# Fetching the rows of the output sum earlier, and moving one-time transfers from SyncE to GpSimd, in a fused attention and feed-forward kernel

## The chip, the cores and the metric

The kernel runs on one core of a Trainium2 chip. The metric is the time of one execution on the device in microseconds (us). A core has five engines that run side by side, each with its own list of instructions in a fixed order: TensorE (PE in the profile, PEld for its weight loads), VectorE (DVE), ScalarE (ACT), GpSimd (POOL) and SyncE (SP), which here only issues transfers. Each engine executes its list in order, so an instruction that waits holds up those behind it on its engine. A framework places the program's instructions on these lists: it draws the waits from what each instruction reads and writes, hands out the buffers of a pool, and may put an instruction earlier than the source has it when its engine and its buffer are free.

## What is computed

The input x has the shape (2, 2048, 256). It is normalised by layer, and attention and a feed-forward net with ternary weights are both applied to the normalised rows; their outputs are added to x.

```python
xn = _layernorm(x, axis=-1)
x = x + _L0_attn_ref(xn, Wq, Wk, Wv, Wo) + _L0_ffn_ref(xn, ...)
# attention: causal, one head of 256, softmax(q k^T / 16) v Wo
# feed-forward, with _tlin(x, w, s) = (x @ w.T) * s and w in {-1, 0, 1}:
h = silu(_tlin(x, w1_w, w1_s)) * _tlin(x, w2_w, w2_s)      # 256 -> 1024
h = gelu(_tlin(h, h1_w, h1_s))                             # 1024 -> 1024
h = gelu(_tlin(h, h2_w, h2_s))                             # 1024 -> 1024
return _tlin(h, w3_w, w3_s)                                # 1024 -> 256
```

## The kernel before

The 4096 rows are cut into eight blocks of 512. The attention part comes first (to about 277 us of the span). It leaves in device memory, for each block, the transposed normalised rows (`xT_d`) and the attention output (`r_d`). Beside it VectorE makes the factors of the first square layer h1, described below, and the weights are looked through; a flag says whether all are whole small numbers. With such weights, as here, the branch `ffn_ternary` runs (from line 691), and all that the change touches is in it. The other branch `ffn` does not run.

**Rounds.** `ffn_ternary` takes two blocks at a time, n and n + 1, in four rounds. In each round `first` computes the gated first layer (TensorE's L736; ScalarE L741 and VectorE L742 empty the banks), then `square` is called twice, for h1 and h2, and then the last layer w3 (L918) is computed for block n + 1 and then block n, with the outer addition (L924, L925) and the transfer out (L926).

**Square layers.** A layer of 1024 by 1024 is computed by seven products in place of eight, from sums and differences of the weight's quarters and of the inputs. `STEPS` lists the seven pairs; the left members (factors) S1 to S4 are sums of weight quarters, A11, A12 and A22 are quarters themselves. A product is 32 matmuls of 128x128 by 128x512 in the trace's groups on L780. The right members are sums of the round's activations: T1 and T2 by VectorE (L756, L762), the two others by GpSimd (L761, L817), each then split into a rounded part (ScalarE, L719) and a rest (VectorE, L720). L762 overwrites what L761 reads, so it follows L761. The results of products are kept or added up by L791, L800 and L801. All eight PSUM banks are in use: the banks of the first layer are those of products 1 and 2.

**Factors.** The factors lie in device memory, in `factors["h1"]` and `factors["h2"]`, seven pieces of 1 MB. `fetch_factors` (the transfers of L885, issued by SyncE) keeps three fetched tiles ahead, so a new fetch can leave when the product three places earlier has ended. The factors of h2 are made within the first round only: `make_h2(c)`, for c from 0 to 3, loads two chunks of 512 KB (L847), forms four sums on GpSimd (L151), and stores them (L851), 1 MB in 512 pieces of 2 KB. It has two staging slots (tag `stg`) and one buffer of sums (tag `sums`, 8 KB per partition), so the next chunk's sums follow the store's landing. `copy_h2` copies the quarters from place to place in device memory (L860), and `load_w3` loads w3 in two chunks (L855) and rounds it on GpSimd (L132). The dictionary `later` says behind which stage of the first layer or which product of h1 each of these is put; `beside` takes it from there:

```python
later = {
    "B11": lambda: make_h2(0), "B12": lambda: copy_h2(0), "B22": lambda: make_h2(1),
    0: lambda: copy_h2(5), 1: lambda: make_h2(2), 2: lambda: copy_h2(6),
    3: lambda: make_h2(3), 5: lambda: load_w3(0), 6: lambda: load_w3(SC // D),
}
```

**Rows of the outer sum.** Behind the second `square`, for each of the round's two blocks, SyncE fetches the attention output (`rt`, L905) and the rows of x (`xt`, L907), 512 KB each, and GpSimd adds them (L908). Each of `rt` and `xt` has one buffer (`bufs=1`), so the fetch of one block's `rt` waits until the block before has been added up. Each of four groups of 128 rows is then scaled into a tile `yt` (L924, three buffers), `rt` is added to it (L925), and `yt` is sent out (L926).

All of these transfers, L847, L851, L855, L860, L885, L905, L907 and L926, and the fetches of the transposed rows (L708) are in SyncE's one list.

Of the kernel before, what the change touches and what calls it, by code (L numbers as in the profile page):

```python
# [9 lines left out]
F32 = mybir.dt.float32  # L10
# [10 lines left out]
P = 128  # L21
# [41 lines left out]
def attn_ffn_kernel(  # L63
# [73 lines left out]
    def rows(n, t):  # L137
        return ds((n % NB) * TB + t * P, P)
# [553 lines left out]
    def ffn_ternary(actx):  # L692
# [13 lines left out]
        def load_xh(n):  # L706
            t = xh1 if n % 2 else xh0
            nc.sync.dma_start(out=t.bitcast(F32).rearrange("p c h t -> p (c h t)"), in_=xT_d[n])  # L708
# [14 lines left out]
        def first(n):  # L723

            B = {k: [None] * HK for k in ("B11", "B12", "B21", "B22")}
            sets = {"B11": [], "T1": [], "B22": [], "T2": []}
            for k in ("B11", "B12", "B22", "B21"):
                xh = xh1 if k[2] == "2" else xh0
                for i in range(HK):
                    o = i + (HK if k[1] == "2" else 0)  # L730
                    name = f"w_{n}_{k}_{i}"
                    p1, p2 = banks(name, 2)
                    for p, w in ((p1, w1_sb), (p2, w2_sb)):
                        for c in range(DC):
                            for a in range(2):
                                nc.tensor.matmul(  # L736
                                    out=p, lhsT=w[:, c, ts(o, P)], rhs=xh[:, c, a, :],
                                    start=(c == 0 and a == 0), stop=(c == DC - 1 and a == 1),
                                )
                    f = B[k][i] = raw(f"f_{name}")  # L740
                    nc.scalar.activation(f, p1, AF.Silu, scale=sc["w1"][:, o : o + 1])  # L741
                    nc.vector.scalar_tensor_tensor(  # L742
                        f, p2, sc["w2"][:, o : o + 1], f, ALU.mult, ALU.mult
                    )
                    if k == "B11":
                        sets[k].append(split(f, f"{n}_{k}_{i}"))
                    elif k == "B12":
                        t1(B, sets, f"{n}", i)
                    elif k == "B22":
                        b22(B, sets, f"{n}", i)  # L750
                beside(k)
            return B, sets


# [9 lines left out]
        def t2(B, sets, name, i):  # L764
            sets["T2"].append(split(B["B22"][i], f"{name}_T2_{i}"))

        def square(layer, n, B, sets, last):

            name = f"{layer}_{n}"
            s = sc[layer]  # L770
            C, nxt = {}, {k: [] for k in ("B11", "B12", "B21", "B22", "T1", "T2")}

            def product(step, out, start):
                right = STEPS[step][1]
                fetch_factors()
                w = factor_tiles.pop(0)
                for o in range(HK):
                    for c in range(HK):
                        for a in range(2):
                            nc.tensor.matmul(  # L780
                                out=out[o], lhsT=w[:, c, ts(o, P)], rhs=sets[right][c][:, a, :],
                                start=(start and c == 0 and a == 0), stop=(c == HK - 1 and a == 1),
                                skip_group_check=True,
                            )
                if layer == "h1":
                    beside(step)

            def kept(banks, k):
                r = [raw(f"k_{name}_{k}_{o}") for o in range(HK)]
                for o in range(HK):  # L790
                    nc.scalar.copy(r[o], banks[o])  # L791
                return r

            def summed(k, banks, r):

                C[k] = r or [raw(f"f_{name}_{k}_{o}") for o in range(HK)]
                for o in range(HK):
                    at = o + (HK if k[1] == "2" else 0)
                    if r:
                        nc.vector.tensor_tensor(r[o], banks[o], r[o], ALU.add)  # L800
                    nc.scalar.activation(  # L801
                        C[k][o], r[o] if r else banks[o], AF.Gelu, scale=s[:, at : at + 1]
                    )
                    if last:
                        nxt[k].append(split(C[k][o], f"{name}_{k}_{o}"))

            X = banks(f"{name}_X", HK)
            product(0, X, True)
            u1 = kept(X, "u1")
            sets["T3"] = [split(B["B12"][i], f"{name}_T3_{i}") for i in range(HK)]  # L810
            Z = banks(f"{name}_Z", HK)
            product(1, Z, True)
            p5 = kept(Z, "p5")
            for i in range(HK):

                t4 = B["B22"][i]
                nc.gpsimd.tensor_tensor(t4, B["B21"][i], t4, ALU.subtract)  # L817
            sets["B21"] = [split(B["B21"][i], f"{name}_B21_{i}") for i in range(HK)]
            product(2, X, False)
            u2 = kept(X, "u2")  # L820
            sets["T4"] = [split(B["B22"][i], f"{name}_T4_{i}") for i in range(HK)]
            product(3, Z, False)
            summed("B12", Z, u2)
            product(4, X, False)
            summed("B22", X, p5)
            Y = banks(f"{name}_Y", HK)
            product(5, Y, True)
            summed("B11", Y, u1)
            if not last:
                for i in range(HK):  # L830
                    nxt["B11"].append(split(C["B11"][i], f"{name}_B11_{i}"))
                for i in range(HK):
                    t1(C, nxt, name, i)
                for i in range(HK):
                    b22(C, nxt, name, i)
            product(6, X, False)
            summed("B21", X, None)
            if not last:
                for i in range(HK):
                    t2(C, nxt, name, i)  # L840
            return C, nxt

        def make_h2(c):
            halves = []
            for k in (c, c + HK):
                t = stgp.tile([P, SC], F32, tag="stg", name=f"stgt_h2_{k}")
                nc.sync.dma_start(out=t, in_=h2[:, k, :])  # L847
                halves.append(t)
            sums = stgp.tile([P, 4, HB], F32, tag="sums", name=f"sums_h2_{c}", bufs=1)
            sums_of_factors(sums, halves, range(4))  # L850
            nc.sync.dma_start(out=factors["h2"][:, 1:5, c, :], in_=sums)  # L851

        def load_w3(c):
            t = stgp.tile([P, SC], F32, tag="stg", name=f"stgt_w3_{c}")
            nc.sync.dma_start(out=t, in_=w3[:, c : c + SC // D, :].rearrange("p c d -> p (c d)"))  # L855
            rounded(w3_sb[:, c : c + SC // D, :].rearrange("p c d -> p (c d)"), t)

        def copy_h2(step):
# [8 lines left out]
            3: lambda: make_h2(3), 5: lambda: load_w3(0), 6: lambda: load_w3(SC // D),  # L867
        }
        assert HK == 4 and HC == 2 * SC // D

        def beside(at):
            if at in later:
                later.pop(at)()


        factor_order = [
# [4 lines left out]
        def fetch_factors():  # L881
            while factor_order and len(factor_tiles) < 3:
# [5 lines left out]
                )  # L888
                factor_tiles.append(w)

        load_xh(1)
        fetch_factors()

        for n in range(0, N, 2):
# [3 lines left out]
            if n + 2 < N:  # L898
                load_xh(n + 2)
                load_xh(n + 3)  # L900
            B, sets = square("h1", n, B, sets, False)
            B, sets = square("h2", n, B, sets, True)
            for m in (n + 1, n):
                rest = op.tile([P, NT, D], F32, tag="r", name=f"rt_{m}", bufs=1)
                nc.sync.dma_start(out=rest, in_=r_d[m].rearrange("p (t d) -> p t d", d=D))  # L905
                xt = op.tile([P, NT, D], F32, tag="x", name=f"xt_{m}", bufs=1)
                nc.sync.dma_start(out=xt, in_=rows_of(m))  # L907
                nc.gpsimd.tensor_tensor(rest, rest, xt, ALU.add)  # L908
                h = sets["B11"] + sets["B21"] if m == n else sets["B12"] + sets["B22"]
                ys = banks(f"y_{m}", NT)  # L910

# [4 lines left out]
                for t, c in order:  # L916
                    for a in range(2):
                        nc.tensor.matmul(  # L918
                            out=ys[t][:, :D], lhsT=h[c][:, a, ts(t, P)], rhs=w3_sb[:, c, :],
                            start=(c == 0 and a == 0), stop=(c == HC - 1 and a == 1),  # L920
                        )
                    if c == HC - 1:
                        y = op.tile([P, D], F32, tag="y", name=f"yt_{m}_{t}")
                        nc.vector.tensor_tensor(y, ys[t][:, :D], s3, ALU.mult)  # L924
                        nc.vector.tensor_tensor(y, y, rest[:, t, :], ALU.add)  # L925
                        nc.sync.dma_start(out=out[m // NB, rows(m, t), :], in_=y)  # L926

    def ffn(actx):

# [192 lines left out]
```

## Time and profile before

| | |
|---|---|
| median of 3 runs | 872.6 us (871.63 to 875.7) |
| profiled execution | 872.97 us, of which the span is 871.1 us |
| granted TensorE clock, mean | 0.993 |
| TensorE busy | 851.1 us |
| VectorE, ScalarE, GpSimd busy | 630.3, 498.2, 236.3 us |
| transfers | 162.51 MB, 187 GB/s on average |

The span goes from the first to the last instruction of the profiled execution. Busy time is the sum of the durations of an engine's instructions; issuing a transfer or waiting is not in it. In the profile's lines "L908" is line 908 of the kernel, `out<-in` are the program's names for what is written and read, and an arrow `<-` ahead of an engine names what ended the idle time. SPq is the list of SyncE. The median time from a transfer's issue to its landing is given with the issues: 4.7 us for a factor tile of 1 MB, 3.7 us for `rt`, 4.3 us for `xt`, 7.7 us for a store of sums, 1.8 us for a transfer out.

### The profile page before, as it was taken

To read this page: it belongs to the slowest core of one execution; us is meant where nothing else is said; L and a number is where in the kernel's file an instruction comes from. 1 tells how busy PE (TensorE), PEld (TensorE's weight loads), DVE (VectorE), ACT (ScalarE), POOL (GpSimd) and SP (SyncE) were. 2 spreads that over 40 slices of the span, in tenths; PEclk is the share of its full clock that TensorE was granted. 3 is DMA by queue.
4 is the path that set the end of the run, shared out by engine and by line. 5 is a ranking of instruction groups with operands and counts; after the bars stand their busy time and mean duration, and the time that the engine had idled before them with its cause. 6 is when DMAs were issued, how large, how long until landed. Compare 5 with 4: busy or idle time off the path is not lost.

```text
span 871.1 us, 12211 instructions
## 1 busy us (share of the span) xinstructions
PE 851.1 (98%) x4280; PEld 720.7 (83%) x4280; DVE 630.3 (72%) x1127; ACT 498.2 (57%) x881; POOL 236.3 (27%) x176
## 2 busy tenths in 40 slices
PE   8999999999989999999999999999999999999996
PEld 5888888988877878888988888988888898888886
DVE  5699688786873995985496596569478648848663
ACT  2547555755644665677266486536657635657670
POOL 4112633201111473540143150025024012402401
PEclk8999999999999999999999999999999999999999
DMA  9867599866792979743424444443444432144412
GB/s 322 312 230 226 176 326 300 298 230 212 243 324 93 375 280 336 273 146 143 139 87 150 146 144 145 149 127 103 145 145 145 146 139 97 49 145 146 145 49 77
DMA packets 63845, 162.51 MB, mean 187 GB/s; under 512 B 6560, under 2 KB 36384, under 8 KB 54560
## 3 DMA queue, kind: packets, MB, share of 16 engines
q1 hardware_dynamic: 58304, 145.92, 48.4%
q10 hardware_dynamic: 5472, 15.73, 5.6%
q8 instruction: 36, 0.59, 0.3%
q14 instruction: 33, 0.27, 0.1%
HBM read 120.21 MB, written 47.71 MB: 193 GB/s over the span
## 4 chain that ended last, share of the span: by engine, by line
PE 61%; DMA 3%; POOL 1%; DVE 1%; issue 0%; SPq 0%; DVEq 0%; POOLq 0%
PE ps_h_X L780 26%; PE ps_h_Z L780 13%; PE ps_w_B L736 10%; PE ps_h_Y L780 7%; PE ps_y L918 6%; DMA stgt_h<-in_ffn_h_w 1%; DMA w_h_S<-factors_h 1%; POOL sums_h L151 1%; DVE f_w_B L762 0%; DMA rt<-r_d 0%; POOL rt L908 0%; DVE h_B L720 0%; DMA out<-yt 0%; POOL f_w_B L761 0%; DVE f_w_B L742 0%
## 5 line engine op out<-in xcount | busy, mean ns | idle before, releaser
L359 PE MATMUL pss<-k,q 128*128 128x512 f32 (+3 forms) x480 | 110.4, 368 | 2.1 <-DVE q L210 1.1
L359 PEld LDWEIGHTS pss<-k,q 128*128 128x128 f32 x480 | 81.6, 189 | 14.9 <-DVE q L210 1.4
L780 PE MATMUL ps_h_X<-h_h_T,w_h_S 128*128 128x512 f32 x384 | 89.1, 389 | 0.3 <-DMA w_h_S<-factors_h 0.3
L780 PEld LDWEIGHTS ps_h_X<-h_h_T,w_h_S 128*128 128x128 f32 x384 | 72.0, 188 | 15.6 <-ACT k_h_u L801 0.7
L438 PE MATMUL po<-v,pT 128*128 128x512 f32 x272 | 79.0, 403 | 3.7 <-ACT pT L418 2.8
L420 POOL TENSOR_TENSOR pT<-e,pT 128x512 fp32r<-128x512 f32 (+3 forms) x30 | 35.6, 1188 | 161.6 <-ACT pT L418 111.0
L908 POOL TENSOR_TENSOR rt<-rt,xt 128x1024 f32<-128x1024 f32 x8 | 19.6, 2453 | 209.9 <-DMA rt<-r_d 209.9
L801 ACT ACTIVATE k_h_u<-k_h_u,h_s_sb 128x512 f32<-128x512 f32 x64 | 46.3, 724 | 41.1 <-DVE k_h_u L800 40.9
L741 ACT ACTIVATE f_w_B<-ps_w_B,w_s_sb 128x512 f32<-128x512 f32 x64 | 43.0, 684 | 43.5 <-PE ps_w_B L736 43.5
L918 PEld LDWEIGHTS ps_y<-w_sbt,h_h_B 128*128 128x128 f32 x512 | 62.0, 192 | 0.3
L918 PE MATMUL ps_y<-w_sbt,h_h_B 128*128 128x256 f32 x512 | 62.1, 283 | 0.0
L736 PE MATMUL ps_w_B<-xh,w_sb 128*128 128x512 f32 x256 | 59.5, 390 | 1.3 <-DVE r L457 1.3
L418 ACT CAST pT<-e 128x512 fp32r<-128x512 f32 (+3 forms) x60 | 32.6, 574 | 48.9 <-DMA e<-d 31.0
L780 PE MATMUL ps_h_X<-h_h_T,w_h_A 128*128 128x512 f32 x256 | 59.3, 389 | 0.0
L780 PE MATMUL ps_h_Y<-h_h_B,w_h_A 128*128 128x512 f32 x256 | 59.3, 389 | 0.0
L736 PE MATMUL ps_w_B<-xh1t,w_sb 128*128 128x512 f32 x256 | 58.7, 389 | 0.0
L438 PEld LDWEIGHTS po<-v,pT 128*128 128x128 f32 x272 | 48.6, 192 | 11.6 <-ACT pT L418 3.3
L736 PEld LDWEIGHTS ps_w_B<-xh,w_sb 128*128 128x128 f32 x256 | 47.8, 188 | 11.2 <-issue 1.5
L780 PEld LDWEIGHTS ps_h_Y<-h_h_B,w_h_A 128*128 128x128 f32 x256 | 48.0, 188 | 10.0
L780 PEld LDWEIGHTS ps_h_X<-h_h_T,w_h_A 128*128 128x128 f32 x256 | 48.0, 188 | 10.0
L736 PEld LDWEIGHTS ps_w_B<-xh1t,w_sb 128*128 128x128 f32 x256 | 48.0, 188 | 10.0
L380 ACT ACTIVATE s<-s,low 128x1024 f32<-128x1024 f32 (+7 forms) x48 | 43.0, 897 | 20.3 <-DVE low L374 19.9
(139 smaller groups left out, 1846.7 us busy)
## 6 DMA issues: line engine op xcount, KB each, us to landing
w_h_S<-factors_h SPq DMA_DIRECT2D x32, 1024.0 KB, 4.7
w_h_A<-factors_h SPq DMA_DIRECT2D x24, 1024.0 KB, 4.7
d<-b SPq DMA_DIRECT2D x18, 512.0 KB, 4.2
e<-d SPq DMA_DIRECT2D x72, 128.0 KB, 4.1
xT_d<-k SPq DMA_DIRECT2D x8, 1024.0 KB, 7.5
stg<-in_ffn_h_w ACTq DMA_DIRECT2D x16, 512.0 KB, 6.6
x<-in_attn_x SPq DMA_DIRECT2D x16, 256.0 KB, 5.5
r_d<-r SPq DMA_DIRECT2D x8, 512.0 KB, 5.3
```

The source lines that it names most:

```text
L151: engine.tensor_tensor(sums[:, i, :], x, y, op)
L359: nc.tensor.matmul(out=ps[:, :w], lhsT=qs[n][:, c, a, ts(t, P)], rhs=ks[m][:, c, b, :w], start=(k == 0), stop=(m < n and k == 3 * DC - 1),)
L380: marks["ACT"] = nc.scalar.activation(st["s"][:, at], st["s"][:, at], AF.Exp, bias=low, accum_out=st["sums"][:, u // UK : u // UK + 1],).ins
L418: nc.scalar.copy(hi, src)
L420: engine.tensor_tensor(lo, src, hi.bitcast(F32), ALU.subtract)
L438: nc.tensor.matmul(out=st["po"], lhsT=pT[:, 0, ts(j, P)], rhs=vs[m][:, j, :, :], start=(m == first and j == 0), stop=False,)
L736: nc.tensor.matmul(out=p, lhsT=w[:, c, ts(o, P)], rhs=xh[:, c, a, :], start=(c == 0 and a == 0), stop=(c == DC - 1 and a == 1),)
L741: nc.scalar.activation(f, p1, AF.Silu, scale=sc["w1"][:, o : o + 1])
L780: nc.tensor.matmul(out=out[o], lhsT=w[:, c, ts(o, P)], rhs=sets[right][c][:, a, :], start=(start and c == 0 and a == 0), stop=(c == HK - 1 ...
L801: nc.scalar.activation(C[k][o], r[o] if r else banks[o], AF.Gelu, scale=s[:, at : at + 1])
L908: nc.gpsimd.tensor_tensor(rest, rest, xt, ALU.add)
L918: nc.tensor.matmul(out=ys[t][:, :D], lhsT=h[c][:, a, ts(t, P)], rhs=w3_sb[:, c, :], start=(c == 0 and a == 0), stop=(c == HC - 1 and a == 1),)
```

## The change

Two things are done in the first round or in each round.

The rows of the outer sum get a function of their own, `rests_of`, that is called behind product 4 (step 3) of `square("h2", ...)`. It fetches `rt` and `xt` of both blocks, n + 1 first, on SyncE, and adds them on GpSimd. Its tiles come from the staging pool: the two `rt` tiles take the two slots of tag `stg`, and one tile for both `xt` takes the buffer of tag `sums`. The addition of L925 now writes its result into the `rt` tile, and the transfer out leaves from there; the tile `yt` holds only the scaled product. The pool `op` loses its tags `r` and `x`.

The loads and stores of `make_h2` and the loads of `load_w3`, 14 transfers in all, are issued by GpSimd in place of SyncE. `copy_h2` stays on SyncE.

For this, `square` takes a dictionary of what is put behind its products, in place of the helper `beside`.

```diff
-                beside(k)
+                if k in later:
+                    later.pop(k)()
...
-        def square(layer, n, B, sets, last):
+        def square(layer, n, B, sets, last, beside):
...
-                if layer == "h1":
-                    beside(step)
+                if step in beside:
+                    beside.pop(step)()
...
-                nc.sync.dma_start(out=t, in_=h2[:, k, :])
+                nc.gpsimd.dma_start(out=t, in_=h2[:, k, :])
...
-            nc.sync.dma_start(out=factors["h2"][:, 1:5, c, :], in_=sums)
+            nc.gpsimd.dma_start(out=factors["h2"][:, 1:5, c, :], in_=sums)
...
-            nc.sync.dma_start(out=t, in_=w3[:, c : c + SC // D, :].rearrange("p c d -> p (c d)"))
+            nc.gpsimd.dma_start(out=t, in_=w3[:, c : c + SC // D, :].rearrange("p c d -> p (c d)"))
...
-        def beside(at):
-            if at in later:
-                later.pop(at)()
...
+        def rests_of(n):
+            xt = stgp.tile([P, 2, NT, D], F32, tag="sums", name=f"xt_{n}", bufs=1)
+            rests = {}
+            for m in (n + 1, n):
+                rests[m] = rest = stgp.tile([P, NT, D], F32, tag="stg", name=f"rt_{m}")
+                nc.sync.dma_start(out=rest, in_=r_d[m].rearrange("p (t d) -> p t d", d=D))
+                nc.sync.dma_start(out=xt[:, m - n], in_=rows_of(m))
+                nc.gpsimd.tensor_tensor(rest, rest, xt[:, m - n], ALU.add)
+            return rests
...
-            B, sets = square("h1", n, B, sets, False)
-            B, sets = square("h2", n, B, sets, True)
+            B, sets = square("h1", n, B, sets, False, later)
+            rests = {}
+            B, sets = square("h2", n, B, sets, True, {3: lambda: rests.update(rests_of(n))})
             for m in (n + 1, n):
-                rest = op.tile([P, NT, D], F32, tag="r", name=f"rt_{m}", bufs=1)
-                nc.sync.dma_start(out=rest, in_=r_d[m].rearrange("p (t d) -> p t d", d=D))
-                xt = op.tile([P, NT, D], F32, tag="x", name=f"xt_{m}", bufs=1)
-                nc.sync.dma_start(out=xt, in_=rows_of(m))
-                nc.gpsimd.tensor_tensor(rest, rest, xt, ALU.add)
+                rest = rests[m]
...
-                        nc.vector.tensor_tensor(y, y, rest[:, t, :], ALU.add)
-                        nc.sync.dma_start(out=out[m // NB, rows(m, t), :], in_=y)
+                        nc.vector.tensor_tensor(rest[:, t, :], y, rest[:, t, :], ALU.add)
+                        nc.sync.dma_start(out=out[m // NB, rows(m, t), :], in_=rest[:, t, :])
```

## The prediction, made before the result was known

> **What bounds the kernel now.** First the page, for the engine that is always at work.
>
> ```profile
> PE   851.1 (98%) x4280; PEld 720.7 (83%) x4280; DVE 630.3 (72%) x1127; ACT 498.2 (57%) x881; POOL 236.3 (27%) x176
> ```
>
> TensorE is busy for all but 20.0 us of the span of 871.1, so no edit that leaves the matmuls alone can win more than lies in those 20. The table of busy time by stage says where they are (start and end of a stretch, its length, then busy time and instructions of each engine, granted clock, DMA share, GB/s).
>
> ```profile
> 277.00:308.00 31.00, 29.71 (x130) 24.34 (x131) 25.07 (x31) 17.00 (x27) 11.31 (x8) 1.00 0.94 347
> 308.00:338.00 30.00, 29.20 (x129) 23.52 (x127) 26.14 (x27) 20.07 (x36) 21.29 (x13) 1.00 0.78 292
> 338.00:426.00 88.00, 88.00 (x449) 75.50 (x450) 60.33 (x84) 51.13 (x86) 28.06 (x17) 1.00 0.55 197
> 426.00:572.00 146.00, 146.00 (x707) 123.53 (x706) 101.85 (x144) 86.66 (x146) 34.89 (x19) 1.00 0.39 137
> 849.00:871.10 22.10, 14.96 (x125) 14.75 (x123) 8.09 (x19) 1.28 (x3) 2.40 (x1) 0.94 0.23 76
> ```
>
> From 338 on TensorE has no idle moment until its last matmul; the fetches of the rows and the waits of GpSimd for them (209.9 us on L908) cost nothing there. The change can act in two places: the entry into the feed-forward part (277 to 338) and the tail (849 to the end). Products are counted from 1 within a square layer. TensorE's timeline shows the entry (start, length, group, and in brackets the idle time before it):
>
> ```profile
> 278.16 7.52 PE L736 MATMUL ps_w_B<-xh,w_sb 128*128 128x512 f32 x32 [1.28 <-DVE r L457]
> 315.63 7.57 PE L780 MATMUL ps_h_Z<-h_T,w_h_S 128*128 128x512 f32 x32 [0.52 <-DVE f_w_B L742]
> 337.99 7.29 PE L780 MATMUL ps_h_X<-h_h_T,w_h_S 128*128 128x512 f32 x31 [0.28 <-DMA w_h_S<-factors_h]
> ```
>
> The chain of waits (start, length, what) has the factor fetch of the entry, a later round, and the tail:
>
> ```profile
> 328.56 9.29 DMA w_h_S<-factors_h
> ...
> 426.14 29.04 PE ps_w_B L736 x128
> ...
> 857.61 3.33 DMA rt<-r_d
> ...
> 861.11 2.40 POOL rt L908
> 863.50 0.02 issue
> 863.53 0.45 DVE yt L925 x2
> 863.98 1.73 DMA out<-yt
> ...
> 865.83 0.44 DVE yt L924
> 866.27 0.02 issue
> 866.29 0.42 DVE yt L925
> ```
>
> In a later round the first layer takes 29.04 and a product 7.25, so layer plus four products take 58.05. In the first round the same work runs from 278.16 to 337.99, which is 59.83: the entry loses 1.78 us. 1.18 of it lies before 315.63 (37.47 against 36.29), where product 2 waits for VectorE to empty the banks; 0.45 is product 5, which could start at 330.29 + 7.25 = 337.54 and waits for its factors. In the tail the rows of the last block are fetched only at 857.61, since the one buffer for them is held until the block before is added up; fetch, sum and a result buffer that waits for its own transfer out put the last addition at 866.71, though TensorE ends at 848.45 + 15.51 = 863.96.
>
> **What the Trainium skill says.** "DMA: Bandwidth & Descriptors", Issuing engines are not separate DMA queues: transfers from any engine run on the same 16 engines, and another issuer saves only sequencer time. So the edit can free SyncE's order, and buys no bandwidth; the entry runs at a DMA share of 0.94. The trace shows only SP's and ACT's queues (q1, q10), no transfer of GpSimd. Same page, Latency and other measured facts: first byte after about 0.6 us from SP or ACT, about 1 us from GpSimd; no row of before can confirm it. "SBUF — State Buffer", Who interferes with whom: a VectorE instruction with two SBUF inputs contends with a GpSimd instruction that reads SBUF. The trace agrees: L756 takes 0.68 us, and 1.79 at 294.10, when the sums of L151 begin.
>
> **The change part by part.**
>
> *Tail.* Both row tiles and their sums are ready before product 7 of the last h2, and a result tile y is no longer held by its transfer out, because the transfer leaves from the row tile. The last L924 then follows TensorE's end as L924 does elsewhere: 0.02 to 0.03 after 863.96, then 0.88 for the pair L924 and L925 (865.83 to 866.71), so 864.87 in place of 866.71: **-1.84 us**. What follows (transfer out and end of program, 871.1 - 866.71 = 4.39) stays. If the addition into row t+1 were made to wait for the transfer out of row t, it would wait until about 865.1 (L925 at 862.5, its end, issue, 1.8 to land), and the gain would still be about 1.1. Next in line is TensorE itself.
>
> *Rows in the other rounds.* Eight fetches of r_d and eight of x (0.43 and 0.39 us of SyncE, 3.7 and 4.3 us to land) and eight sums of 2.40 move from behind the square layers to product 4 of h2, or earlier when their slots are free. In round 1 the staging slots are free after the last copy of w3 (361.51 + 1.51) and the sums' slot after its store lands (360.3), and the rows are needed at 413.7: some 50 us for about 14. On SyncE four issues, 1.64 us, go ahead of factor fetches that leave when a product ends, 14.5 us before they are needed, and land in 4.7: 9.8 us of cover. On GpSimd two sums, 4.8 us, have no other work behind them within h2. Cost nothing; without the cover at most 1.64 us a round. What no longer happens is that the rows of block 1 are fetched at 291.75 to 294.27 and 312.10, 1.5 MB in the crowded entry.
>
> *SyncE without GpSimd's transfers.* The factor tile of product 5 can be fetched when product 2 ends (323.04). Today the issue waits behind L847 and L851, which wait for the sums of GpSimd (17.6 us on L847 between 320 and 375), until 328.56. Freed, it lands at 323.1 + 7.1 to 9.3, by 333, before 337.54: **-0.45 us**. What is late next is nothing until product 2 of h2.
>
> *GpSimd with its own transfers.* Eight loads of h2 rows, four stores of sums, two loads of w3: 14 issues, off SyncE (0.33 to 1.94 us each there) and onto an engine that is busy 11.3 of 31 and 21.3 of 30 us in the entry. No row of before prices one. Low end: 0.4 us, the difference of the two first bytes in the skill. High end: 6.1, as if a store of 512 pieces were wholly written out by GpSimd before any of it moved (6.1 is what the store takes on SP's queue). I take 1.0 each, the skill's figure, an estimate. Queued behind them are L761 and L817, for which VectorE (L762) and then TensorE wait. Before, the first sums wait until 293.9 for rows issued at 284.01, behind three 1 MB fetches on one queue; on a queue of their own they may start up to about 2.5 us earlier (my estimate: half of the 4.9 that the first of the three takes to land), and the store's issue then takes 1.0 back ahead of L761. I take the two as equal, **0**, between -1.18 (the early loss is gone) and +2.
>
> The other wait is the loop sums, store, next sums, since there is one sums buffer. Stores 2, 3 and 4 leave at 327.58, 339.49 and 351.06; the fourth takes 9.2 us, the fetch for product 2 of h2 leaves at 360.34, lands 4.9 later at 365.24, and TensorE needs it at 367.27. **The slack is 2.03 us.** Each of three stores gains at least 0.4 of latency and up to 1.0 of issue, +1.2 to +3; against that the fourth no longer shares one queue with the fetch of 350.12 and the w3 loads (9.2 against 6.1 when alone). I take +2 - 2 = 0 of shift and no stall.
>
> *Sum.* 1.84 + 0.45 = 2.29 less. The profiled execution took 872.97, its span 871.1 and 1.87 around it: 872.97 - 2.29 = 870.7. The median of the three runs is 872.6, which gives 870.3. I predict **870.6**, between them.
>
> **The rivals.**
> (1) *The entry closes too*: GpSimd's sums come earlier, L761 is on time, all 1.78 us go. 872.6 - 1.84 - 1.78 = **869.0**. For it: L761 starts at 300.41, the moment the sums end. Against it: the same sums then slow VectorE earlier.
> (2) *Partly paid back*: the sums of the second chunk, at 319 to 327.6 today, move up into 303 to 315, where TensorE waits for VectorE directly. Four to six additions at 1.79 in place of 0.69 are 4.4 to 6.6 us of VectorE, about half of it in front of L742: +2.8, so about **873.1**.
> (3) *Slower: issue on GpSimd stretches the loop of sums and stores.* Place: product 2 of h2 in round 1. Three stores in series, each longer by e; beyond the slack of 2.03 TensorE stands still for 3e - 2.03. It eats the gain from e = (2.29 + 2.03) / 3 = 1.44 us, and is slower by 0.5% from e = 2.9. With e = 3, half the high end, +9 - 2.03 - 2.29 = +4.7: **877.3**. For it: the loop has the smallest cover of all, and a store is 512 pieces of 2 KB. Against it: separate queues, 1.5 MB less traffic.
> (4) *The rows aren't fetched early in the last round* (the staging slots are not free in time): then only 0.45 is won, 872.1; they are held until round 3 has written out, about 24 us after its last layer begins as in round 1, so to about 727, and needed at 857; I give it little.
>
> **How the numbers follow.** Forecast (869.8 to 871.6) 0.50; rival 1 0.14; rival 2 0.15; rival 3 0.17; rival 4 0.04. About 0.5%, 4.4 us, is what a measurement of this kernel can tell from no change. Faster than 868.2 needs all of rival 1 and more, since 3.6 us is all that the two places hold: 0.06, for a run that comes out low. Slower than 877.0 is the upper part of rival 3, and some of the unknown price of 14 issues: 0.15. Within: 0.79. For 8 in 10 the range goes from just under rival 1, 868.8, to 876.5, which leaves out the upper two thirds of rival 3; likeliest case alone 869.8 to 871.6.
>
> **What would show it.** Tail: no GpSimd sum after 849, the last L925 ending about 0.9 us after the last matmul, no wait of L924 for a transfer out. SyncE: the fetch for product 5 issued at about 323, no wait of it for sums. GpSimd: first sums at 291 to 294, L761 within 2 us of 300. Loop: the fetch for product 2 of h2 landing before that product can start. The prediction is wrong if TensorE shows idle time over 1 us between 338 and 380, if VectorE's L742 comes later than before in front of product 2, or if the program's end grows when GpSimd has transfers of its own.

## The result, and the profile after

The changed kernel takes **878.43 us** (875.38 to 882.54, 18 runs) against 874.09 for the kernel before (870.16 to 875.95, 18 runs on the same chip): ratio 1.006, 95% interval [1.0044, 1.0075]. It is slower by 0.6%, where 870.6 was forecast. The profiled execution took 877.46 us, its span is 875.3 and its mean granted clock 0.993, as before.

TensorE does the same work in a longer span (in the lines of after, L780 has become L782, L847 L849, L851 L853 and L885 L883). On the page of after:

```profile
PE 852.2 (97%) x4280; PEld 720.7 (82%) x4280; DVE 639.5 (73%) x1127; ACT 499.0 (57%) x881; POOL 240.0 (27%) x190
```

The table of busy time by stage, after, says where it now stands still (columns as before):

```profile
308.00:338.00 30.00, 30.00 (x134) 24.83 (x133) 24.49 (x27) 20.05 (x35) 19.53 (x16) 1.00 0.67 249
338.00:426.00 88.00, 82.89 (x402) 69.10 (x401) 64.80 (x81) 51.00 (x86) 32.91 (x23) 1.00 0.61 221
426.00:572.00 146.00, 146.00 (x706) 123.53 (x706) 102.63 (x144) 86.86 (x146) 34.05 (x18) 1.00 0.39 137
849.00:875.30 26.30, 20.45 (x151) 19.39 (x149) 9.90 (x21) 4.86 (x9) 0.00 (x0) 0.96 0.14 44
```

The entry from 308 to 338 is closed (30.00 of 30, 29.20 before). The stretch 338 to 426, which had no idle moment, has 5.11 us of it; the later rounds still have none. In the tail GpSimd does nothing any more, as planned. TensorE's timeline, after, shows the 5.11 us in one place, products 2 and 3 of h2 in round 1:

```profile
359.15 7.42 PE L782 MATMUL ps_h_X<-h_h_B,w_h_A 128*128 128x512 f32 x32
370.06 7.52 PE L782 MATMUL ps_h_Z<-h_h_T,w_h_S 128*128 128x512 f32 x32 [3.49 <-DMA w_h_S<-factors_h]
377.89 1.40 PE L782 MATMUL ps_h_X<-h_h_T,w_h_S 128*128 128x512 f32 x5 [0.31 <-DMA w_h_S<-factors_h]
379.64 0.73 PE L782 MATMUL ps_h_X<-h_h_T,w_h_S 128*128 128x512 f32 x2 [0.35 <-DVE h_h_T L720]
381.32 5.95 PE L782 MATMUL ps_h_X<-h_h_T,w_h_S 128*128 128x512 f32 x25 [0.96 <-DVE h_h_T L720]
387.11 7.42 PE L782 MATMUL ps_h_Z<-h_h_B,w_h_S 128*128 128x512 f32 x32
```

Product 2 waits 3.49 for its factors. Products 2 and 3 then take 387.11 - 370.06 = 17.05 in place of 14.50.

**The sum, span against span**, in us: the attention part is 0.68 shorter (first layer at 277.48, before 278.16; other profiles have 275.9 to 281.6, a scatter of executions). From there to product 1 of h2 nothing is won (81.67 against 81.69: product 5's wait is gone, but the first layer takes 30.89 in place of 29.40). Product 2's start costs +3.65 (10.91 after product 1's, before 7.26), products 2 and 3 cost +2.55, the way to the last matmul nothing, and the tail -1.29. The sum is +4.2, and 875.3 - 871.1 = 4.2.

In the tail, after, the last addition follows the last matmul (end 869.45) at once:

```profile
869.49 0.42 DVE L931 TENSOR_TENSOR yt<-ps_y,s 128x256 f32<-128x256 f32 x1 [1.03 <-PE ps_y L925]
869.95 0.43 DVE L932 TENSOR_TENSOR rt<-yt,rt 128x256 f32<-128x256 f32 x1
```

What delayed product 2 is seen on SyncE's and GpSimd's lines. First before, the third store, the sums behind it and the fetch for product 2:

```profile
339.49 0.37 SPq L851 DMA_DIRECT2D factors_h<-sums_h  x1
...
345.74 1.30 POOL L151 TENSOR_TENSOR sums_h<-stgt_h 128x512 f32<-128x512 f32 x1 [6.28 <-DMA factors_h<-sums_h]
...
360.34 14.53 SPq L885 DMA_DIRECT2D w_h_S<-factors_h  x4
```

Then after, GpSimd's timeline (with the wait in brackets) and SyncE's:

```profile
339.20 0.77 POOL L853 DMA_DIRECT2D factors_h<-sums_h  x1
...
348.91 1.28 POOL L151 TENSOR_TENSOR sums_h<-stgt_h 128x512 f32<-128x512 f32 x1 [8.42 <-DMA factors_h<-sums_h]
351.32 1.30 POOL L151 TENSOR_TENSOR sums_h<-stgt_h,stgt_h 128x512 f32<-128x512 f32 x1 [1.12 <-DMA stgt_h<-in_ffn_h_w]
...
356.52 0.77 POOL L853 DMA_DIRECT2D factors_h<-sums_h  x1
...
371.59 5.75 POOL L898 TENSOR_TENSOR rt<-rt,xt 128x1024 f32<-128x1024 f32 x2 [0.48 <-DMA xt<-in_attn_x]
```

```profile
337.58 7.57 SPq L883 DMA_DIRECT2D w_h_A<-factors_h  x2
363.80 0.32 SPq L896 DMA_DIRECT2D rt<-r_d  x1
364.34 0.32 SPq L883 DMA_DIRECT2D w_h_S<-factors_h  x1
```

Two things are to be seen. The third store, issued at 339.20, holds up the next sums until 348.91: 9.7 us, where before it was 6.25 (339.49 to 345.74). And the fetch for product 2 of h2 (364.34) now has a fetch of rows directly ahead of it, and two of x behind it. In the trace the last store had landed at 363.55; the fetch of rows, which waits for its staging slot, held the factor fetch for another 0.79 us (before: 0.08). The issues themselves are short: 0.77 for a store, 0.55 for a load.

### The profile page after: what moved, and what is told of

Its sections match the earlier page's. It is cut to its first block, busy times and chain, and to the rows that moved or that the text cites. A ratio compares the mean times of both kernels' runs of the same rounds, so it can differ in the third digit from the quotient of the medians.

```text
span 875.3 us, 12206 instructions
## 1 busy us (share of the span) xinstructions
PE 852.2 (97%) x4280; PEld 720.7 (82%) x4280; DVE 639.5 (73%) x1127; ACT 499.0 (57%) x881; POOL 240.0 (27%) x190
## 4 chain that ended last, share of the span: by engine, by line
PE 78%; DVE 8%; DMA 6%; ACT 3%; issue 2%; POOL 1%; SPq 1%; ACTq 0%; DVEq 0%; POOLq 0%
PE ps_h_X L782 25%; PE ps_h_Z L782 12%; PE ps_w_B L736 12%; PE ps_y L925 7%; PE ps_h_Y L782 6%; PE pss L359 5%; PE po L438 4%; PE pv L331 2%; PE po L443 2%; DMA e<-d 2%; PE pq L315 2%; DMA stg<-in_ffn_h_w 2%; DMA d<-b 1%; DVE b L250 1%; DVE stg L525 1%
## 5 line engine op out<-in xcount | busy, mean ns | idle before, releaser
L782 PE MATMUL ps_h_X<-h_h_T,w_h_S 128*128 128x512 f32 x384 | 89.7, 390 | 1.6 <-DVE h_h_T L720 1.3
L782 PEld LDWEIGHTS ps_h_X<-h_h_T,w_h_S 128*128 128x128 f32 x384 | 71.8, 188 | 17.6 <-DVE h_h_T L720 2.2
L736 PE MATMUL ps_w_B<-xh,w_sb 128*128 128x512 f32 x256 | 59.8, 390 | 2.8 <-DVE f_w_B L742 1.5
L925 PEld LDWEIGHTS ps_y<-w_sbt,h_h_B 128*128 128x128 f32 x512 | 62.0, 192 | 0.3
L925 PE MATMUL ps_y<-w_sbt,h_h_B 128*128 128x256 f32 x512 | 62.1, 283 | 0.0
L782 PE MATMUL ps_h_Y<-h_h_B,w_h_A 128*128 128x512 f32 x256 | 59.3, 389 | 0.0
L782 PE MATMUL ps_h_X<-h_h_T,w_h_A 128*128 128x512 f32 x256 | 59.3, 389 | 0.0
L782 PEld LDWEIGHTS ps_h_X<-h_h_T,w_h_A 128*128 128x128 f32 x256 | 48.0, 188 | 10.0
L782 PEld LDWEIGHTS ps_h_Y<-h_h_B,w_h_A 128*128 128x128 f32 x256 | 48.0, 188 | 10.0
```

Of the source, the lines that this page charges most:

```text
L736: nc.tensor.matmul(out=p, lhsT=w[:, c, ts(o, P)], rhs=xh[:, c, a, :], start=(c == 0 and a == 0), stop=(c == DC - 1 and a == 1),)
L782: nc.tensor.matmul(out=out[o], lhsT=w[:, c, ts(o, P)], rhs=sets[right][c][:, a, :], start=(start and c == 0 and a == 0), stop=(c == HK - 1 ...
L925: nc.tensor.matmul(out=ys[t][:, :D], lhsT=h[c][:, a, ts(t, P)], rhs=w3_sb[:, c, :], start=(c == 0 and a == 0), stop=(c == HC - 1 and a == 1),)
```

## The experiments

Theories, as the expectations letter them. A: GpSimd's own transfers stretch the loop of sums and stores, that is the loss, and the rows alone bring the tail's gain. B: the rows, ahead of and beside the fetch for product 2 of h2. C: in runs 1 and 2, that both are needed, since each alone leaves slack; in run 10 the letter stands for the loop as the cause. D and E split A: the factor fetches that SyncE now issues earlier push GpSimd's stores back (D), or GpSimd's transfers are slow by themselves (E). Ratios are to the kernel before, with 95% intervals. To keep the attention part's scatter out, times of round 1 are given **from the start of the first layer**: before, the stores leave at 22.3, 49.4, 61.3 and 72.9, the fetch at 82.2, its factors land at 87.1, and product 2 starts at 89.0. (The prediction, from the chain of waits, had the slack between the last two at 2.03.)

**1. Rows alone.** The edit is to the changed kernel: all transfers stay on SyncE.

```diff
-                nc.gpsimd.dma_start(out=t, in_=h2[:, k, :])
+                nc.sync.dma_start(out=t, in_=h2[:, k, :])
```

(and so for the stores and w3.)

> The changed kernel with its 14 one-time transfers issued by SyncE again; the rows of the outer sum stay as changed (staging memory, behind product 4 of h2). Theory A (GpSimd's own transfers stretch the loop of sums and stores, and that is the loss): faster than before by the tail, 1.3 to 1.8 us, so about 872.5 beside 874.1; the last store lands near 360 as before, and product 2 of h2 starts without a wait over 1 us. Theory B (the fetch of the rows waits on SyncE for the staging slots, in front of the factors of product 2 of h2, and that is the loss): slower than before by about 4 us, with TensorE idle at products 2 and 3 of h2. Theory C (both are needed, since each alone leaves slack): within 1 us of before.

Measured: 879.22, ratio 1.0045 [1.003, 1.0061]. A falls as the whole account, since the rows alone lose too, and the place is a new one. TensorE's timeline of this kernel:

```profile
348.31 9.12 PE L782 MATMUL ps_h_Y<-h_h_B,w_h_A 128*128 128x512 f32 x32 [3.69 <-DMA w_h_A<-factors_h]
```

Its SyncE list says why:

```profile
337.19 0.33 SPq L849 DMA_DIRECT2D stgt_h<-in_ffn_h_w  x1
338.57 0.37 SPq L853 DMA_DIRECT2D factors_h<-sums_h  x1
339.03 0.46 SPq L883 DMA_DIRECT2D w_h_A<-factors_h  x1
```

The framework laid the list out anew: the fetch for product 6 of h1, which left at 330.49 before, now stands behind a load and a store that wait for GpSimd's sums.

**2 to 4. GpSimd's part alone**, then its loads alone, then its stores alone, on the kernel before:

```diff
-                nc.sync.dma_start(out=t, in_=h2[:, k, :])
+                nc.gpsimd.dma_start(out=t, in_=h2[:, k, :])
...
-            nc.sync.dma_start(out=factors["h2"][:, 1:5, c, :], in_=sums)
+            nc.gpsimd.dma_start(out=factors["h2"][:, 1:5, c, :], in_=sums)
```

(and so for the loads of w3.)

> The kernel before with its 14 one-time transfers (loads and stores of the h2 sums, loads of w3) issued by GpSimd; the rows of the outer sum are left as before. Theory A: slower than before by about 6 us (the changed kernel's 4.3 and the tail gain that is missing), 879 to 881; the last sums end near 356 and not 351, and product 2 of h2 waits 3 to 4 us for its factors. Theory B: faster by 0.5 us, since SyncE is freed and nothing waits for staging slots. Theory C: about 2 to 4 us slower.

> The kernel before with only the ten loads issued by GpSimd; the stores of the sums stay on SyncE. Theory A in the form that the start of a GpSimd transfer is late while SyncE's queue has one in flight: the loads start 2 to 4 us late, the next sums wait for the second load, and the loop is longer by 1 to 3 us a turn; slower than before by 2 to 4 us. In the form that only the stores matter (they stand alone in the loop): within 1 us of before.

> The kernel before with only the four stores of the sums issued by GpSimd; the loads stay on SyncE. Theory A, late start: each store starts 2 to 4 us late if a fetch is in flight, but it goes out ahead of no load of its own queue; slower by 1 to 4 us. In the form that only the loads matter: within 1 us of before, or faster by about 0.5, since SyncE no longer waits for sums at the stores.

Measured: both 880.9, ratio 1.0088 [1.0063, 1.0113]; loads alone 879.64, 1.0066 [1.004, 1.0091]; stores alone 888.75, 1.0157 [1.0123, 1.019]. The fourth store leaves at 83.3, 81.3 and 87.3, and product 2 of h2 waits 7.7, 2.8 and 7.7 us. The first time is what A said (879 to 881), though with twice the wait that it gave; the stores alone lose far more than the 1 to 4 us expected. GpSimd's timeline of that kernel:

```profile
344.09 1.28 POOL L151 TENSOR_TENSOR sums_h<-stgt_h,stgt_h 128x512 f32<-128x512 f32 x1 [11.25 <-DMA factors_h<-sums_h]
...
362.12 1.29 POOL L151 TENSOR_TENSOR sums_h<-stgt_h,stgt_h 128x512 f32<-128x512 f32 x1 [11.80 <-DMA factors_h<-sums_h]
```

With SyncE free of the stores, its loads and factor fetches leave within 0.3 us of them and land sooner (the fetch issued at 332.17 lands at 342.73, the store of 332.07 at 344.01), and a store that took 6.1 us takes 12. That is the stretched loop of A. Loads alone do harm too: the second of a pair lands 11 us after its issue.

**5. GpSimd's part alone, without the factor fetches of products 6 and 7 of h1 in round 1.**

```diff
+                if layer == "h1" and n == 0 and step in (5, 6):
+                    factor_tiles.append(factor_tiles[-1])
+                    continue
```

The two products use product 5's factors again: the kernel leaves two of the layer's seven factors out in round 1.

> The second experiment (GpSimd issues the 14 transfers) with the factor fetches of products 6 and 7 of h1 in round 1 left out: these two products use the factor tile of product 5 again, so part of the computation is not the reference's. Two fetches of 1 MB are gone from SyncE's queue while GpSimd's loop runs. Theory D (SyncE, freed of its waits, sends fetches that have time to spare ahead of the stores and loads of the loop, and these wait for the same 16 engines): a turn of the loop falls from 17 to 19 us to about 12, the last sums end near 352, product 2 of h2 waits under 1 us for its factors, and the time comes to within 1 us of before, 874 to 876. Theory E (a transfer of GpSimd is slow by itself): the turn stays at 15 us or more, product 2 of h2 waits 4 us or more, and the time stays at 879 to 882.

Measured: 879.5, ratio 1.006 [1.0038, 1.0082]; product 2 of h2 still waits 5.9 us. The total says E, but the trace says less. One fetch was left in the first of the two turns, and lay across the second load. GpSimd's timeline of this kernel:

```profile
339.60 1.29 POOL L151 TENSOR_TENSOR sums_h<-stgt_h 128x512 f32<-128x512 f32 x1 [6.27 <-DMA factors_h<-sums_h]
344.78 1.29 POOL L151 TENSOR_TENSOR sums_h<-stgt_h,stgt_h 128x512 f32<-128x512 f32 x1 [3.90 <-DMA stgt_h<-in_ffn_h_w]
```

In the next turn, with no fetch near it, the store held up the sums for 6.8 us (349.29 to 356.06). Without fetches in the way, then, GpSimd costs a store 0.5 us and not 3.5; but the whole turn still takes 14.0 us against 11.6, because a load's issue (0.55) stands ahead of the store's and the additions take 1.62 to 1.74 each, beside VectorE's work, in place of 1.30. How much of the loss is D and how much E stays open.

**6 and 7. Two buffers for the sums**, in the changed kernel and in the rows-only one: the next sums no longer wait for a store.

```diff
-            sums = stgp.tile([P, 4, HB], F32, tag="sums", name=f"sums_h2_{c}", bufs=1)
+            sums = stgp.tile([P, 4, HB], F32, tag="sums", name=f"sums_h2_{c}", bufs=2)
```

(and so for the tile of both `xt`, which shares the tag, so that the fetches of x can leave earlier too.)

> The changed kernel with two buffers of sums in place of one (the 8 KB that the rows left free in the output pool). The next sums no longer wait for the store before. If the loop of sums and stores is what holds product 2 of h2, its wait goes below 1 us, and the time falls by 4 to 6 us, to 873 to 875, below or level with before. If the fetch of the rows in front of the factors of product 2 of h2 holds it (theory B), the wait of 3.5 us stays, and so does the time, 878 to 880. If the loads and not the stores set the loop, something between: 2 to 3 us less.

> The first experiment (rows in staging memory, all transfers on SyncE) with two buffers of sums. There product 6 of h1 waited 3.7 us for a fetch that stood in SyncE's list behind a load that waits for sums. With two buffers the sums run ahead of their stores, so that wait falls below 1 us: 4 us less than the first experiment, and faster than before by the tail and the entry, 1.3 to 2.5 us, so 872.5 to 874. If the order of the list is the loss whatever the sums do, product 6 or another waits 2 us or more still, and the time is 877 to 880.

Measured: the changed kernel 874.89, ratio 1.0007 [0.9988, 1.0026]; rows-only 878.62, ratio 1.0048 [1.0024, 1.0073]. So the loop is part of the changed kernel's loss and not of the rows-only one's, whose product 6 still waits 4.0 us. In the changed kernel the fetch now leaves at 82.2, as before, and yet product 2 waits:

```profile
371.86 7.54 PE L782 MATMUL ps_h_Z<-h_h_T,w_h_S 128*128 128x512 f32 x32 [2.29 <-DMA w_h_S<-factors_h]
```

The fetch takes 7.9 us to land instead of 4.9, with the rows beside it. That brought theory B back.

**8. The last round alone.** In the kernel before, only block 6 (the last one worked) gets its `rt` in a staging slot and adds into it, issued after the last factor fetch. The edit in part:

```diff
+                if m == N - 2:
+                    rest = stgp.tile([P, NT, D], F32, tag="stg", name=f"rt_{m}")
+                    with tc.issue_after(marks["SP"]):
+                        nc.sync.dma_start(out=rest, in_=r_d[m].rearrange("p (t d) -> p t d", d=D))
```

> The kernel before, where only the rows of the very last block are fetched into a staging slot, tied behind the last factor fetch, and the sum is written into them; SyncE's list of round 1 is that of before. If the tail gain of the changed kernel is real and independent of the entry: faster by 1.3 to 1.8 us (the end of the program 5.3 to 5.8 us after the last matmul in place of 7.1), ratio near 0.998. If the tail was moved by something else: no difference.

Measured: 872.62, ratio 0.998 [0.9967, 0.9994]. The tail after the last matmul is 5.6 us, in place of 7.1. The tail's gain needs nothing else of the change.

**9. Rows alone, SyncE's list kept in its order.** The third store and the loads after it are issued after the fetch for product 6, and the rows after a later fetch. The edit in part:

```diff
+                with tc.issue_after(marks["SP"]):
+                    marks.pop("store")()
```

> The rows part alone, with all transfers on SyncE as in the kernel before, but with SyncE's list held in the order that it had before: the store of the third sums and the loads of the fourth chunk are issued after the factor fetch of product 6 of h1, and the rows' fetches after the last factor fetch that has been asked for by then. If the loss of the rows-only kernel was the new order of the list (a fetch standing behind a store that waits for sums), product 6 of h1 waits under 0.5 us in place of 3.7, nothing new waits in round 1, and the gain of the tail (1.3) is left: ratio 0.996 to 0.999, about 872. If the rows cost something by themselves (slots that they hold, 1 MB more in the entry), the loss stays: ratio 1.003 or more, about 877.5, with a wait elsewhere between 338 and 426.

Measured: 872.42, ratio 0.9972 [0.9955, 0.9989]. Product 6 does not wait, and product 2 of h2 waits 0.44. The loss of the rows-only kernel was the order of the list (both parts of it were put back at once, so their shares are not told apart), the rows cost nothing that shows beyond it, and this kernel is the fastest of the study, level with runs 8 and 11 within the intervals.

**10 and 11. The changed kernel with the rows' fetches later**, and the same with two buffers for the sums.

```diff
+                with tc.issue_after(marks["SP"]):
+                    nc.sync.dma_start(out=rest, in_=r_d[m].rearrange("p (t d) -> p t d", d=D))
+                    nc.sync.dma_start(out=xt[:, m - n], in_=rows_of(m))
```

> The changed kernel, with the rows' fetches issued after a later factor fetch instead of ahead of that of product 2 of h2. If the loop of sums and stores is what holds that product (theory C), its fetch leaves at the landing of the last store, at most 0.3 us sooner, and lands at most about 0.7 us quicker because no rows share the way: the wait at product 2 of h2 goes from 3.5 to about 2.5, and product 3's 1.3 goes; ratio about 1.003 to 1.005. If the rows standing ahead of the fetch were the main cause (theory B), the wait falls under 1 us and the ratio to about 0.999.

> The changed kernel with two buffers for the sums, and with the rows' fetches after a later factor fetch. With two buffers alone a wait of 2.3 us stayed at product 2 of h2, and its fetch took about 8 us to land in place of 4.9. If that rest came from the rows' transfers beside the fetch, the wait is gone (under 0.3 us), the gains of the tail (1.3) and of product 5 (0.45) stay, less 1.3 at the first layer: ratio 0.996 to 0.999. If the rest was the loop's, a wait of about 2 us stays and the ratio is about 1.001, as with two buffers alone.

Measured: 873.88, ratio 0.9992 [0.9977, 1.0007], and 872.94, ratio 0.9985 [0.997, 1.0]. The first is what B said, and C had given 1.003 to 1.005; in the second a wait of 0.37 is left at product 2. SyncE's and TensorE's lines of the first of the two:

```profile
366.06 12.80 SPq L885 DMA_DIRECT2D w_h_S<-factors_h  x4
```

```profile
370.97 7.54 PE L782 MATMUL ps_h_Z<-h_h_T,w_h_S 128*128 128x512 f32 x32 [0.70 <-DMA w_h_S<-factors_h]
378.35 7.42 PE L782 MATMUL ps_h_X<-h_h_T,w_h_S 128*128 128x512 f32 x32
```

Product 2 waits 0.70 in place of 3.49, product 3 not at all. The expectation went wrong on two points: the fetch left 2.4 us sooner (84.4 against 86.9), where 0.3 was the most expected, and products 2 and 3 take 2.4 less (14.64 against 17.05), where 1.3 was.

**12. The changed kernel a second time**, for a second profile of round 1.

> The changed kernel a second time, for a second profile of round 1 and no time. In its first profile the fourth store left 79.0 us after the start of the first layer, with the rows' fetches later 77.3. If that difference belongs to the place of the rows, the store leaves at about 79 again and the wait at product 2 of h2 is 3.0 to 3.8; if it is scatter from one execution to the next, the store leaves at about 77 to 78, and the wait is 1.5 to 3, of which the rows ahead of the fetch make 1.5. The waits of product 3, about 1.6 in sum, should come again in both cases, since the rows' sums stand on GpSimd ahead of what product 3 needs.

One execution, 878.23 us. The fourth store leaves at 77.3 here, as with the rows later, so the 1.7 us that the first profile had more was scatter. The wait at product 2 is 3.7 all the same, and not the 1.5 to 3 expected. SyncE's and TensorE's lines of this execution:

```profile
361.36 0.32 SPq L896 DMA_DIRECT2D rt<-r_d  x1
363.21 0.32 SPq L883 DMA_DIRECT2D w_h_S<-factors_h  x1
363.58 1.05 SPq L897 DMA_DIRECT2D xt<-in_attn_x  x2
```

```profile
370.96 9.12 PE L782 MATMUL ps_h_Z<-h_h_T,w_h_S 128*128 128x512 f32 x32 [3.74 <-DMA w_h_S<-factors_h]
```

The fetch leaves at 84.5, as in run 10 (84.4), but product 2 starts 7.75 us after its issue, where run 10 had 4.91: with the same store and the same fetch, the rows beside it cost 2.84 us. Of product 3's waits, expected again at about 1.6, one of 0.48 came; instead product 2 itself took 9.12 in place of 7.5 (see the last section), so that products 2 and 3 took 17.01, as long as in the first profile.

**Four kernels in a square.** The ratios of the changed kernel with one or two buffers of sums, and with the rows early or late:

| | rows early | rows late |
|---|---|---|
| one buffer of sums | 1.0060 [1.0044, 1.0075] | 0.9992 [0.9977, 1.0007] |
| two buffers | 1.0007 [0.9988, 1.0026] | 0.9985 [0.997, 1.0] |

Against two buffers and late rows, the loop alone costs 0.0007, the early rows alone 0.0022, both together 0.0075 (6.6 us). The intervals of single ratios reach 0.0015 to 0.0019 each way, so only the last of the three is clearly a loss. **Two delays use one slack of 2 us:** the late loop takes all of it, and early rows lengthen the fetch's landing by up to 3 us. The waits at product 2, in one profile of each and two of the last, are 0.37 with neither, 0.70 with the loop, 2.29 with the rows, and 3.49 and 3.74 with both. Only with both does the wait grow by about 1 us beyond the two added up, and do products 2 and 3 take 17.0 us in place of 14.6. This is the thought of C in the first runs, though the two kernels built there to test it (1 and 2) lost in other ways.

## Why the prediction was wrong

Two terms that were put at nothing failed: the rows, on SyncE and on GpSimd, and the loop of sums and stores.

**Rows in the other rounds: this step failed.** It said that the four issues go ahead of factor fetches that leave when a product ends, with 9.8 us of cover, and cost nothing. The list of after has the first of them ahead of the one fetch that does not leave when a product ends, but when the last store has landed, and that has 2.03 us of cover by the prediction's own count. In run 12 the rows make 2.84 us of the wait of 3.74; in the first profile they make 1.4, half by standing ahead of the fetch (0.79 against 0.08) and half by a longer landing (5.58 against 4.88). In rounds 2 to 4, where the fetches do leave when a product ends, the step held: TensorE has no idle moment there. "Behind product 4 of h2" in the source was read as the place in SyncE's list; the prediction had noted that rows may go earlier when their slots are free, and did not ask whose fetch they would then meet.

**GpSimd's sums of the rows: this failed too.** "On GpSimd two sums have no other work behind them within h2" looks for a queue at product 4; the sums came sooner, ahead of L817's four sums, which the trace of before has from 370.66, and the harm came by another way. The two sums (5.75 us from 371.59) now run beside VectorE's splits of the activations for product 3. VectorE's timeline of after, and then of before:

```profile
372.18 9.09 DVE L720 TENSOR_TENSOR h_h_T<-k_h_p,h_h_T 128x512 fp32r<-128x512 f32 x4
```

```profile
369.90 2.49 DVE L720 TENSOR_TENSOR h_h_T<-k_h_p,h_h_T 128x512 fp32r<-128x512 f32 x4
```

Four splits take 9.09 us in place of 2.49, and product 3 waits for them. The two beside the rows' sums take 2.89 each, the two beside the sums that follow on GpSimd 1.77, and alone one takes 0.68. The prediction cited the rule of the Trainium skill ("SBUF — State Buffer", Who interferes with whom), with which these lengths agree, and used it for the entry only. In run 10, with the rows' sums after 393, products 2 and 3 take 14.64 in place of 17.05. Early rows do not always meet the splits: in run 6 the first sum is over at 371.54, ahead of product 2, and the second comes at 382.24, and the two products take 14.63.

**The loop of sums and stores: right place, wrong sum.** "+2 - 2 = 0 of shift and no stall" took 0.4 to 1.0 more for each of three stores and 2 less for the fourth. Run 12 has, for the turn from the third store to the fourth, 16.6 us against 11.6: the store lands 3.5 later, the additions take 1.1 more, the load's issue ahead of the store about 0.5. The fourth store does gain its 2 (7.1 against 9.2). The second store leaves 1.9 sooner and the turn after it takes 1.2 more, so the fetch leaves 2.3 late (84.5 against 82.2), which is the slack and 0.3 over; run 10, where nothing else is in the way, waits 0.70. The term that was mis-sized is the third store: in the packets of the first profile it and the load ahead of it begin to move at 341.68, 3.0 us after the load's issue, when the factor fetch of 337.58 is nearly through (its last packet at 342.15). Before, that fetch stood behind the store in SyncE's list (341.95), although its slot had been free since the product's end. The prediction counted SyncE's freedom as a gain (product 5) and overlooked that the old order was what gave the stores the way. It had the sentence for it: another issuer buys no bandwidth (the Trainium skill, "DMA: Bandwidth & Descriptors", Issuing engines are not separate DMA queues), and the third store's 9.6 us to land in place of 6.1 agrees.

**Price of an issue on GpSimd.** Taken as 1.0, measured 0.55 for a load and 0.77 for a store. It was not the cost.

**Product 5: right.** Its fetch left at 323.08 and it did not wait. **Entry: "0" was half a microsecond too good**: the first layer takes 1.49 more, product 2 comes 0.68 later, and by product 5 it is even with before (59.9 and 59.8), so the 0.45 of product 5 was used up there.

**Tail: right in kind.** Forecast -1.84, measured -1.29. The last addition ends 0.93 after the last matmul, as worked out (0.91); the part behind it took 4.92 where 4.39 was taken as fixed. In the kernels with this tail the time from last matmul to end is 5.6 to 6.4, so half a microsecond is scatter here.

**Rival 3** had the place, the sign and nearly the size (877.3), but by one mechanism only, and the nearness of its number is luck: it has three stores 3 us longer each, where the fetch left 2.3 late in all (run 12). With the loop alone, run 10 is level with the kernel before; the rows were missing in it, which were given 0, and 1.64 us at most. It had a chance of 0.17, and its 877.3 lay outside the range, which ended at 876.5.

**Open.** GpSimd's part alone (run 2) loses more than the same part with late rows (run 10): its third store leaves at 67.3 and not 60.7. The two differ in round 1 by the rows' place, which in run 2 is the crowded entry. Which of transfers and GpSimd's sum of 2.40 us among the layer's work does it was not tried. In the turn that follows, the two traces differ by a collision: in run 2 the second load (327.35) has a factor fetch 1.0 us behind it and takes 12.1 us to land; in run 10 the fetch leaves 4.0 us behind it, and it takes 7.6.

## What to carry to other kernels

A list that waits is also an order of priority: before transfers are taken out of it, ask which of those behind them will now go first, and who needs the ones that fall back. Look for the transfer that leaves on a landing instead of on an engine's progress: here it had 2 us of slack, where the prediction counted 9.8 for the others. Move nothing ahead of or beside it, and add up all the parts of a change that use the same slack before calling any of them covered. A prefetch should be tied to the place where it is wanted, since the framework puts it where its buffers come free: the gain here was to be had from one block's rows.

## What was not expected of the hardware

A stall can cost more than itself. After waits of 3.69, 3.74, 4.01, 5.89, 7.68 and 7.74 us (runs 1, 12, 7, 5, 4 and 2) the next product took 9.12, 9.12, 8.88, 9.49, 9.45 and 9.71 us; after 3.49, 2.75 and 2.29 (the first profile of after, runs 3 and 6) it took 7.52, 7.54 and 7.54. In run 12 the granted clock is 0.81 from 370 to 373 and 0.62 from 373 to 376; in the first profile of after it stays at 1.00. The Trainium skill ("TensorE: Matmul & The Clock Gate", What's actually happening) says that the clock falls after an idle window of about 3.4 us. The traces agree with that in size: 3.49 did not bring it down and 3.69 did; where the limit lies between or beside them they do not show.

A transfer of GpSimd begins to move 1.25 us after its issue when no other transfer is under way (355.97, after), and 4.3 us after it where 1.45 MB of SyncE's move in between (282.49, after). It is not peculiar to GpSimd: in run 5 a factor fetch of SyncE, issued at 333.29 behind 2 MB of GpSimd's, began at 337.80.
